# Two LSTMs in a decoder kernel: gates in two parts, cell and output gate transposed in place of h, inputs as three bf16 numbers, and a written-out order of half steps

## The chip, the cores and the metric

The kernel runs on one core of a Trainium2 chip. The metric is the device time of one execution in microseconds (us). The engines are named as in the profile: PE is TensorE, with its weight loads listed apart as PEld; DVE is VectorE, ACT is ScalarE, POOL is GpSimd, and SP issues most of the DMAs. A name such as L612 is a line of the kernel before.

## The reference, cut to what matters

The whole program is a decoder of four layers, each with self attention, cross attention and a feed-forward part, over x of 8 batches x 112 steps x 256. The change lies in the first sublayer. Its queries and keys come out of two LSTMs that read the same normalised x. Each has 256 units, so 1024 gate columns, and runs 112 steps one after the other:

```python
xW = jnp.einsum('bsd,gd->sbg', x, Wih) + b
def step(carry, xt):
    h, c = carry
    gates = xt + h @ Whh.T
    i, f, g, o = jnp.split(gates, 4, axis=-1)
    c = jax.nn.sigmoid(f) * c + jax.nn.sigmoid(i) * jnp.tanh(g)
    h = jax.nn.sigmoid(o) * jnp.tanh(c)
    return ((h, c), h)
...
hq = _lstm(hidden_states, Wih_q, Whh_q, b_q)
hk = _lstm(hidden_states, Wih_k, Whh_k, b_k)
```

Everything is float32. What follows (two small MLPs, attention, the other eleven sublayers) is untouched by the change.

## The kernel before, in words

`decoder` calls the twelve sublayers one after the other. `l0_attn` (L517) normalises x, transposes it (`ln_T_mm`), runs `lstm` (L559), then makes the values (L533, L534) and the attention. All instructions are issued through a tile framework that places the waits and, unless told otherwise, picks each engine's order by its own priorities.

In `lstm` a step's 8 batches x 1024 gate columns are laid out so that all 128 partitions work. `_gates` (L72) permutes the weights' columns at build time: column block j (0 to 3) of 256 columns holds 64 units of each gate, in the order i, f, o, g. A matmul with 32 stationary columns puts block j on partitions 32j to 32j + 31, so four matmuls fill a PSUM tile g of 128 x 256 (line L612, loops over the two halves c of h and the four blocks j). The 8 batches use 8 of the 32 partitions of each block.

The input part, xW, is made in blocks of 16 steps. `inputs(m, l, half)` (L580) multiplies 128 rows (8 batches x 16 steps) by 512 of the 1024 columns on PE and adds the bias on DVE into the SBUF tile `xw` (L585). `from_inputs(t, l)` (L587) brings the rows of step t into a fresh g: its stationary operand `pick[:, t % 16, :]` is a 0/1 matrix that selects 8 of the 128 rows (L590). PE does float32 matmuls as two instructions each, and here the moving operand is float32, 256 columns wide.

A time step of one LSTM (l = 0 is q, 1 is k) is then: 16 matmul instructions of h into g (L612); the inputs of the next step into the other g (L621, two PSUM buffers per LSTM); one sigmoid over 192 columns (L623) and one tanh over 64 (L624) on ACT; three DVE operations for the cell (L629 to L632); tanh of the cell on ACT (L634); h = o * tanh(c) on DVE (L636), with batches on partitions; DVE's transpose of 32 x 32 blocks, which gives hT with units on partitions (L638), the next step's stationary operand; and POOL's copy of its 8 batch columns to `hs` (L639), which keeps all steps. The two LSTMs are independent and alternate. The first 16 steps' inputs are made ahead of the loop; the other 24 blocks of 512 columns (`later`, L603) go one after every fourth step (L640).

Of the kernel before, what the change touches and what calls it, by code (L numbers as in the profile page):

```python
# [22 lines left out]
BF16 = mybir.dt.bfloat16  # L23
AF = mybir.ActivationFunctionType
ALU = mybir.AluOpType
AX = mybir.AxisListType
ET = mybir.EngineType
PSUM = bass.MemoryType.PSUM

P = 128  # L30
S, NB, D = 112, 8, 256
T = S * NB
# [39 lines left out]
def _gates(w):  # L72

    i, f, g, o = np.split(w, 4, axis=0)
    a = np.stack([i, f, o, g]).reshape(4, 2, 4, 32, *w.shape[1:])
    return np.moveaxis(a, 2, 0).reshape(1024, *w.shape[1:])


# [11 lines left out]
def _weights(inp):  # L90
    def g(layer):
        return lambda name: inp[f"{layer}_{name}"]

    a, xa, f = g("L0_attn"), g("L0_xattn"), g("L0_ffn")
    blobs = [
        [("l0a_ih_q", _fm(_gates(a("Wih_q")).T))],
        [("l0a_hh_q", _fm(_gates(a("Whh_q")).T))],
        [("l0a_ih_k", _fm(_gates(a("Wih_k")).T))],
        [("l0a_hh_k", _fm(_gates(a("Whh_k")).T))],
        [("l0a_b_q", _row(_gates(a("b_q")))), ("l0a_b_k", _row(_gates(a("b_k"))))],  # L100
# [228 lines left out]
class _Kernel:  # L329
# [229 lines left out]
    def lstm(self, hs, xs, ps0):  # L559

        nc, tc = self.nc, self.tc
        G = range(4)
        whh = [self.w("l0a_hh_q", 2), self.w("l0a_hh_k", 2)]
        wih = [self.w("l0a_ih_q", 2), self.w("l0a_ih_k", 2)]  # L570
        bias = [self.w("l0a_b_q"), self.w("l0a_b_k")]
        pick = self.c("pick").rearrange("p (r m) -> p r m", r=16)
        with tc.tile_pool(name="ps_lstm", bufs=2, space=PSUM) as ps, tc.tile_pool(
            name="lstm", bufs=2
        ) as work, tc.tile_pool(name="lstm_c", bufs=1) as cpool:

            xw = self.t(cpool, [P, 2, S // 16, 1024], "xw")
            cell = [self.t(cpool, [P, 64], f"cell{l}") for l in range(2)]

            def inputs(m, l, half):  # L580
                cols = slice(512 * half, 512 * half + 512)
                pm = self.t(ps0, [P, 512], "mm")
                steps = [xs[:, k, m, :, :].rearrange("p b r -> p (b r)") for k in range(2)]
                self.mm(pm, [(x, wih[l][:, k, cols]) for k, x in enumerate(steps)])
                nc.vector.tensor_tensor(xw[:, l, m, cols], pm, bias[l][:, cols], ALU.add)  # L585

            def from_inputs(t, l):  # L587
                g = self.t(ps, [P, 256], f"g{l}")
                for j in G:
                    nc.tensor.matmul(  # L590
                        g[32 * j : 32 * j + 32, :],
                        pick[:, t % 16, :],
                        xw[:, l, t // 16, 256 * j : 256 * j + 256],
                        start=True,
                        stop=t == 0,
                        skip_group_check=True,
                    )
                return g

            for l in range(2):  # L600
                for half in range(2):
                    inputs(0, l, half)
            later = [(m, l, half) for m in range(1, S // 16) for l in range(2) for half in range(2)]  # L603
            gs = [from_inputs(0, l) for l in range(2)]
            hT = [None, None]
            for t in range(S):
                for l in range(2):
                    g = gs[l]
                    if t > 0:
                        for c in range(2):  # L610
                            for j in G:
                                nc.tensor.matmul(  # L612
                                    g[32 * j : 32 * j + 32, :],
                                    hT[l][:, c, :],
                                    whh[l][:, c, 256 * j : 256 * j + 256],
                                    start=False,
                                    stop=c == 1,
                                    skip_group_check=True,
                                )
                    if t + 1 < S:  # L620
                        gs[l] = from_inputs(t + 1, l)  # L621
                    sg = self.t(work, [P, 256], f"sg{l}")
                    nc.scalar.activation(sg[:, :192], g[:, :192], AF.Sigmoid)  # L623
                    nc.scalar.activation(sg[:, 192:], g[:, 192:], AF.Tanh)  # L624
                    ig, fg, og, gg = (sg[:, 64 * i : 64 * i + 64] for i in range(4))
                    if t == 0:
                        nc.vector.tensor_tensor(cell[l], ig, gg, ALU.mult)
                    else:
                        nc.vector.tensor_tensor(cell[l], cell[l], fg, ALU.mult)  # L629
                        tmp = self.t(work, [P, 64], f"tmp{l}")  # L630
                        nc.vector.tensor_tensor(tmp, ig, gg, ALU.mult)
                        nc.vector.tensor_tensor(cell[l], cell[l], tmp, ALU.add)  # L632
                    th = self.t(work, [P, 64], f"th{l}")
                    nc.scalar.activation(th, cell[l], AF.Tanh)  # L634
                    h = self.t(work, [P, 64], f"h{l}")
                    nc.vector.tensor_tensor(h, og, th, ALU.mult)  # L636
                    hT[l] = self.t(work, [P, 2, 32], f"hT{l}")
                    nc.vector.transpose(hT[l].rearrange("p c b -> p (c b)"), h)  # L638
                    nc.gpsimd.tensor_copy(hs[:, t, l, :, :], hT[l][:, :, :NB])  # L639
                if t % 4 == 2 and later:  # L640
                    inputs(*later.pop(0))

    def l0_attend(self, hs, vv):
        nc, tc, w = self.nc, self.tc, self.w
# [1352 lines left out]
```

## Time and profile before

| | |
|---|---|
| median of 3 runs | 2508.41 us (2505.84 to 2514.92) |
| the profiled execution | 2510.18 us, span of its instructions 2508.4 us |
| mean granted TensorE clock | 0.933 |
| busy over the span: PE, PEld, DVE, ACT, POOL | 2223.4, 1343.6, 1460.0, 834.6, 212.9 us |
| first input product of the LSTMs ready (L585) | 25.8 us |
| first product from h (L612) to last copy to hs (L639) | 34.6 to 433.1 us |
| matmuls of h (L612) | 3552 instructions of 384 ns |
| matmuls of the inputs into g (L590) | 1792 of 379 ns |
| sigmoid (L623), tanh (L624), tanh of the cell (L634) | 224 each, 331, 218 and 258 ns |
| h (L636), its transpose (L638), POOL's copy (L639) | 224 each, 225, 245 and 217 ns |

The duration of a matmul in such a table runs from its start until its result is written; matmuls overlap, so busy time overstates what PE does. In the timeline each row gives start, length, engine, line, operation, the tile written and the tiles read, the shape, and in brackets how long the engine had idled and what released it. Rows that follow one another are merged (x16), with the time from the first start to the last end.

### The profile page before, as it was taken

Reading aid. Unit: us, or ns where it says so; the run is one execution under the profiler, and the core shown is the slowest. Engines: PE = TensorE matmul, PEld = TensorE weight load, DVE = VectorE, ACT = ScalarE, POOL = GpSimd, SP = SyncE. Lnnn points to the kernel's source line nnn. Section 1 sums busy time; section 2 is a strip of 40 time slices with the busy share of each in tenths; the row PEclk is TensorE's granted clock in tenths of the full one; section 3 lists DMA queues with packets and bytes.
Section 4 is the critical chain, followed back from the end, with each engine's and each line's share of the span. In section 5 each row is a group of like instructions: output and inputs, shape, how many; then the busy total and the mean of one; then the engine's idle time right before and its main releaser. Section 6 shows DMA issues by size and latency. Waiting matters only on the chain.

```text
span 2508.4 us, 43509 instructions
## 1 busy us (share of the span) xinstructions
PE 2223.4 (89%) x17192; PEld 1343.6 (54%) x17192; DVE 1460.0 (58%) x3879; ACT 834.6 (33%) x2276; POOL 212.9 (8%) x412
## 2 busy tenths in 40 slices
PE   6999999989989889999998887899999999799942
PEld 3444444657655656655666444456655556556622
DVE  4555656555544656763588664767660042656698
ACT  2333333111221246751012122367521111356621
POOL 0111111000001110000112231100000000100000
PEclk9999999786899999999999997999999999899966
DMA  4000001000010000001000001000111000000000
GB/s 182 2 2 2 2 19 63 1 17 1 17 51 1 14 18 2 18 18 42 34 1 34 18 18 59 34 2 1 52 51 50 35 17 1 1 1 2 2 0 15
DMA packets 10731, 56.42 MB, mean 22 GB/s; under 512 B 1833, under 2 KB 3625, under 8 KB 5536
## 3 DMA queue, kind: packets, MB, share of 16 engines
q1 hardware_dynamic: 8304, 45.03, 5.0%
q0 software_dynamic: 2080, 7.07, 0.8%
q8 instruction: 137, 2.24, 0.4%
q10 hardware_dynamic: 144, 1.54, 0.1%
q14 instruction: 66, 0.54, 0.1%
HBM read 52.69 MB, written 0.92 MB: 21 GB/s over the span
## 4 chain that ended last, share of the span: by engine, by line
PE 67%; DVE 21%; issue 5%; ACT 4%; DMA 1%; POOL 1%; DVEq 0%; ACTq 0%; POOLq 0%
PE mm L378 33%; PE gu L378 6%; PE g L612 6%; PE tr L1031 6%; PE sc L378 5%; PE av L378 3%; PE av L1047 2%; DVE xnm L1021 2%; DVE rot L1326 1%; ACT sg L623 1%; PE s L378 1%; ACT th L634 1%; DVE hT L638 1%; PE tr L477 1%; DVE h L636 1%
## 5 line engine op out<-in xcount | busy, mean ns | idle before, releaser
L612 PE MATMUL g<-w,hT 128*32 128x256 f32 x3552 | 237.4, 384 | 25.8 <-DVE hT L638 24.4
L1024 ACT ACTIVATE xe<-sc,xnm 112x375 f32<-112x375 f32 x384 | 215.6, 580 | 29.1 <-DVE xnm L1021 29.1
L1031 PEld LDWEIGHTS tr<-cst,xe 112*125 112x125 f32 x1152 | 157.2, 187 | 108.8 <-ACT xkT L982 30.0
L378 PE MATMUL mm<-xnT,w 128*128 128x448 f32 x432 | 191.3, 580 | 20.3 <-DVE qT L1329 4.5
L1031 PE MATMUL tr<-cst,xe 112*125 112x112 f32 x1152 | 197.8, 291 | 11.4 <-DVE xoT L1074 6.5
L1021 DVE TENSOR_REDUCE xnm<-sc 112x1 f32<-112x375 f32 x384 | 184.4, 541 | 29.2 <-PE sc L378 29.0
L378 PE MATMUL mm<-hT,w 128*128 128x448 f32 x512 | 193.0, 539 | 0.0
L612 PEld LDWEIGHTS g<-w,hT 128*32 128x32 f32 x3552 | 95.7, 109 | 167.5 <-DVE hT L638 124.6
L1039 DVE COPY xeT<-tr 125x336 f32<-125x336 f32 x192 | 97.4, 507 | 98.1 <-PE tr L1031 90.5
L378 PEld LDWEIGHTS mm<-hT,w 128*128 128x128 f32 x512 | 97.1, 190 | 94.4 <-issue 94.4
L378 PEld LDWEIGHTS mm<-xnT,w 128*128 128x128 f32 x432 | 80.5, 199 | 109.1 <-issue 55.8
L590 PE MATMUL g<-xw,cst 128*32 128x256 f32 x1792 | 138.7, 379 | 0.0
L378 PE MATMUL mm<-w,oT 128*112 128x256 f32 x416 | 119.8, 445 | 21.2 <-DVE oT L1506 13.7
L378 PE MATMUL mm<-w,hT 128*112 128x256 f32 x576 | 132.6, 389 | 0.0
L1037 ACT COPY xeT<-tr 125x336 f32<-125x336 f32 x192 | 85.3, 444 | 127.6 <-PE tr L1031 127.6
L378 PE MATMUL gu<-xnT,w 128*128 128x448 f32 x320 | 124.4, 544 | 1.7 <-DVE hT L1171 1.2
L378 PEld LDWEIGHTS mm<-w,hT 128*112 128x112 f32 x576 | 103.6, 182 | 27.6 <-issue 4.9
L378 PEld LDWEIGHTS mm<-w,oT 128*112 128x112 f32 x416 | 82.9, 208 | 52.4 <-DVE oT L1506 14.9
L623 ACT ACTIVATE sg<-g 128x192 f32<-128x192 f32 x224 | 74.2, 331 | 105.2 <-PE g L612 93.4
L634 ACT ACTIVATE th<-cell 128x64 f32<-128x64 f32 x224 | 57.7, 258 | 147.0 <-DVE cell L632 146.9
L455 DVE TENSOR_TENSOR x<-mm,x 112x256 f32<-112x256 f32 x64 | 27.1, 423 | 126.2 <-PE mm L378 126.2
L636 DVE TENSOR_TENSOR h<-sg,th 128x64 f32<-128x64 f32 x224 | 50.4, 225 | 84.9 <-ACT th L634 84.9
(375 smaller groups left out, 3744.5 us busy)
## 6 DMA issues: line engine op xcount, KB each, us to landing
w<-in_w SPq DMA_DIRECT2D x35, 1024.0 KB, 4.9
raw<-in_wq POOLq DMA_DIRECT2D x3, 1024.0 KB, 5.2
wi<-in_wint POOLq DMA_DIRECT2D x3, 768.0 KB, 5.9
w<-in_w SPq DMA_DIRECT2D x2, 896.0 KB, 16.6
w<-in_w SPq DMA_DIRECT2D x2, 768.0 KB, 4.1
ctxT<-in_ctxT ACTq DMA_DIRECT2D x1, 1500.0 KB, 7.8
cx<-in_ctx POOLq DMA_DIRECT2D x1, 1500.0 KB, 20.9
w<-in_w SPq DMA_DIRECT2D x2, 512.0 KB, 3.5
```

The source lines that it names most:

```text
L378: self.nc.tensor.matmul(out, lhsT, rhs, start=i == 0, stop=i == len(pairs) - 1)
L590: nc.tensor.matmul(g[32 * j : 32 * j + 32, :], pick[:, t % 16, :], xw[:, l, t // 16, 256 * j : 256 * j + 256], start=True, stop=t == 0, sk ...
L612: nc.tensor.matmul(g[32 * j : 32 * j + 32, :], hT[l][:, c, :], whh[l][:, c, 256 * j : 256 * j + 256], start=False, stop=c == 1, skip_group ...
L623: nc.scalar.activation(sg[:, :192], g[:, :192], AF.Sigmoid)
L634: nc.scalar.activation(th, cell[l], AF.Tanh)
L636: nc.vector.tensor_tensor(h, og, th, ALU.mult)
L1021: nc.vector.tensor_reduce(nm, sc, AX.X, ALU.max, negate=True)
L1024: nc.scalar.activation(e, sc, AF.Exp, bias=nm, accum_out=sums[b][:, at : at + 1])
L1031: nc.tensor.transpose(tp[:CH, i * S : (i + 1) * S], e[:, i * CH : (i + 1) * CH], self.ident[:S, :S])
L1037: nc.scalar.copy(eT, src)
L1039: nc.vector.tensor_copy(eT, src)
L1047: nc.tensor.matmul(avs[b][32 * j : 32 * j + 32, c * S : (c + 1) * S], values[b % 2][:CH, i, 4 * c + j, :], eTs[b, c, j][:, i, :], start=i ...
```

## The change

It does five things, all of them for the LSTMs.

1. The gates' order in a block becomes g, i, f, o, and each g splits into two PSUM tiles of 128 columns in banks of their own: part 0 with g and i, part 1 with f and o. The products of h run part by part, so that part 0 is finished first. ACT does four operations of 64 columns in place of one of 192 and one of 64. Each of the four tiles (two LSTMs, two parts) has one buffer.
2. h is no longer transposed. DVE transposes the cell and the output gate instead, tanh is taken of the transposed cell, and h is formed with units on partitions, on 2 x 8 columns. The stationary operand of h's products has 8 columns in place of 32.
3. The inputs xW are stored as a sum of three bf16 numbers, hi, mid and lo, which POOL splits off after DVE's bias add (two copies, two subtractions). `pick` is bf16, and `from_inputs` does three bf16 matmuls for each block and part in place of one float32 matmul for each block. `xw` is a ring of two tiles for each LSTM.
4. The later input products come in 96 pieces of 128 columns in place of 24 of 512: one in each half step of l = 0, and one more in l = 1 every eighth step, until they are done.
5. The order of PE, DVE and ACT is written out (`manual_schedule`): half step n is step n // 2 of LSTM n % 2, and `state`, the last part of a half step (tanh of the cell and h), is issued within the next half step, behind that one's first two activations and its tmp. POOL's order is left to the framework.

```diff
-    a = np.stack([i, f, o, g]).reshape(4, 2, 4, 32, *w.shape[1:])
+    a = np.stack([g, i, f, o]).reshape(4, 2, 4, 32, *w.shape[1:])
...
-        with tc.tile_pool(name="ps_lstm", bufs=2, space=PSUM) as ps, tc.tile_pool(
+        with tc.tile_pool(name="ps_lstm", bufs=1, space=PSUM) as ps, tc.tile_pool(
...
+            pick = self.t(cpool, [P, 16, 32], "pick", BF16)
+            nc.vector.tensor_copy(pick, self.c("pick").rearrange("p (r m) -> p r m", r=16))
...
-            def inputs(m, l, half):
-                cols = slice(512 * half, 512 * half + 512)
-                pm = self.t(ps0, [P, 512], "mm")
+            def inputs(m, l, cols):
+                pm = self.t(ps0, [P, 512], "mm")[:, : cols.stop - cols.start]
...
-                nc.vector.tensor_tensor(xw[:, l, m, cols], pm, bias[l][:, cols], ALU.add)
+                if (m, l) not in xws:
+                    xws[m, l] = self.t(work, [P, 3, 1024], f"xw{l}", BF16)
+                hi, mid, lo = (xws[m, l][:, i, cols] for i in range(3))
+                x = self.t(work, [P, 512], "x")[:, : cols.stop - cols.start]
+                nc.vector.tensor_tensor(x, pm, bias[l][:, cols], ALU.add)
+                nc.gpsimd.tensor_copy(hi, x)
+                nc.gpsimd.tensor_tensor(x, x, hi, ALU.subtract)
+                nc.gpsimd.tensor_copy(mid, x)
+                nc.gpsimd.tensor_tensor(lo, x, mid, ALU.subtract)
+
+            def product(g, lhsT, rhs, l, part, start, stop):
+                for j in G:
+                    at = 256 * j + 128 * part
+                    nc.tensor.matmul(
+                        g[32 * j : 32 * j + lhsT.shape[1], :], lhsT, rhs[:, at : at + 128],
+                        start=start, stop=stop, skip_group_check=True,
+                    )
 
             def from_inputs(t, l):
-                g = self.t(ps, [P, 256], f"g{l}")
...
+                gs = [self.t(ps, [P, 512], f"g{l}{part}")[:, :128] for part in range(2)]
+                for part, g in enumerate(gs):
+                    for i in range(3):
+                        xw = xws[t // 16, l][:, i, :]
+                        product(g, pick[:, t % 16, :], xw, l, part, i == 0, t == 0 and i == 2)
+                return gs
...
-            later = [(m, l, half) for m in range(1, S // 16) for l in range(2) for half in range(2)]
...
+            later = [
+                (m, l, slice(128 * q, 128 * q + 128))
+                for m in range(1, S // 16) for l in range(2) for q in range(8)
+            ]
+            hT, turned = [None, None], [None, None]
+
+            def state(t, l):
+
+                cT, oT = turned[l]
+                th = self.t(work, [P, 2, NB], f"th{l}")
+                nc.scalar.activation(th, cT[:, :, :NB], AF.Tanh)
+                hT[l] = self.t(work, [P, 2, NB], f"hT{l}")
+                nc.vector.tensor_tensor(hT[l], oT[:, :, :NB], th, ALU.mult)
+                nc.gpsimd.tensor_copy(hs[:, t, l, :, :], hT[l])
+
+            with tc.manual_schedule(engines={ET.PE, ET.DVE, ET.Activation}):
+
+                gs = [from_inputs(0, 0), None]
+                for n in range(2 * S):
+                    t, l = n // 2, n % 2
+                    for part, g in enumerate(gs[l]):
+                        for c in range(2):
+                            if t > 0:
+                                product(g, hT[l][:, c, :], whh[l][:, c, :], l, part, False, c == 1)
+                    ga, gb = gs[l]
+                    if n + 1 < 2 * S:
+                        gs[1 - l] = from_inputs((n + 1) // 2, 1 - l)
...
+                    nc.scalar.activation(flat[:, :64], ga[:, :64], AF.Tanh)
+                    nc.scalar.activation(flat[:, 64:128], ga[:, 64:], AF.Sigmoid)
+                    tmp = self.t(work, [P, 64], f"tmp{l}") if t > 0 else cell[l]
+                    nc.vector.tensor_tensor(tmp, ig, gg, ALU.mult)
+                    if n > 0:
+                        state((n - 1) // 2, 1 - l)
+                    nc.scalar.activation(flat[:, 128:192], gb[:, :64], AF.Sigmoid)
+                    nc.scalar.activation(flat[:, 192:], gb[:, 64:], AF.Sigmoid)
                     if t > 0:
                         nc.vector.tensor_tensor(cell[l], cell[l], fg, ALU.mult)
...
                         nc.vector.tensor_tensor(cell[l], cell[l], tmp, ALU.add)
...
-                    nc.vector.tensor_tensor(h, og, th, ALU.mult)
-                    hT[l] = self.t(work, [P, 2, 32], f"hT{l}")
-                    nc.vector.transpose(hT[l].rearrange("p c b -> p (c b)"), h)
-                    nc.gpsimd.tensor_copy(hs[:, t, l, :, :], hT[l][:, :, :NB])
-                if t % 4 == 2 and later:
-                    inputs(*later.pop(0))
+                    turned[l] = [self.t(work, [P, 2, 32], f"{i}T{l}") for i in "co"]
+                    nc.vector.transpose(turned[l][0].rearrange("p c b -> p (c b)"), cell[l])
+                    nc.vector.transpose(turned[l][1].rearrange("p c b -> p (c b)"), og)
+                    if later and t > 16 * later[0][0] - 18 and (l == 0 or t % 8 == 4):
+                        inputs(*later.pop(0))
+                state(S - 1, 1)
```

## The prediction

> **What bounds the kernel now.** I read the windows view first. The change touches one stage only, the two LSTMs, whose recurrence runs from 34.6 to 433.1 us; columns are length, then busy time (and count) of PE, PE's weight loads, DVE, ACT, POOL, then granted clock, DMA share, GB/s.
>
> ```profile
> 34.60:433.10 398.50, 372.69 (x5420) 171.26 (x5421) 239.69 (x1137) 154.85 (x666) 48.03 (x221) 1.00 0.04 12
> ```
>
> PE looks 94% busy, but a matmul's record holds its pipeline latency. So I went on to the timeline, which shows one whole time step (start, length, engine, line):
>
> ```profile
> 106.67 1.07 PE L612 MATMUL g<-w,hT 128*32 128x256 f32 x16 [0.26 <-DVE hT L638]
> 107.56 0.61 PE L590 MATMUL g<-xw,cst 128*32 128x256 f32 x8
> 107.87 0.33 ACT L623 ACTIVATE sg<-g 128x192 f32<-128x192 f32 x1 [0.40 <-PE g L612]
> 108.09 0.22 ACT L624 ACTIVATE sg<-g 128x64 f32<-128x64 f32 x1
> 108.23 0.23 DVE L629 TENSOR_TENSOR cell<-cell,sg 128x64 f32<-128x64 f32 x1
> 108.37 0.22 DVE L631 TENSOR_TENSOR tmp<-sg 128x64 f32<-128x64 f32 x1
> 108.63 0.22 DVE L632 TENSOR_TENSOR cell<-cell,tmp 128x64 f32<-128x64 f32 x1
> 108.94 0.26 ACT L634 ACTIVATE th<-cell 128x64 f32<-128x64 f32 x1 [0.63 <-DVE cell L632]
> 109.23 0.23 DVE L636 TENSOR_TENSOR h<-sg,th 128x64 f32<-128x64 f32 x1 [0.38 <-ACT th L634]
> 109.59 0.24 DVE L638 STREAM_TRANSPOSE hT<-h 128x64 f32<-128x64 f32 x1
> 109.89 1.07 PE L612 MATMUL g<-w,hT 128*32 128x256 f32 x16 [0.23 <-DVE hT L638]
> ```
>
> Each link starts as the one above ends: latency of one LSTM's chain sets the step, 109.89 - 106.67 = 3.22 us; the other LSTM runs in its gaps. So a half step (one LSTM, one step) costs 1.61 us. 111 x 3.22 = 357 us. The rest is the later input products (L584), 24 blocks of 512 columns:
>
> ```profile
> 112.27 0.61 PE L590 MATMUL g<-xw,cst 128*32 128x256 f32 x8
> 112.81 1.98 PE L378 MATMUL mm<-w,xs 128*128 128x512 f32 x4
> 114.73 0.42 PE L612 MATMUL g<-w,hT 128*32 128x256 f32 x4
> ```
>
> Matmuls from hT began at 109.89, 111.38 (gaps alternate 1.49 and 1.73), so the next was due at 113.11; it began at 114.73: 1.62 us, times 24 = 39 us. 357 + 39 = 396 against 398.5 measured.
>
> Last I looked for POOL beside DVE, since the change gives POOL work:
>
> ```profile
> 2151.98 1.13 POOL L1739 TENSOR_TENSOR eT<-eT,cst 112x448 f32<-112x448 f32 x1 [5.77 <-ACT eT L1737]
> 2152.36 1.23 DVE L1739 TENSOR_TENSOR eT<-eT,cst 112x448 f32<-112x448 f32 x1 [2.04 <-ACT eT L1737]
> ...
> L1739 DVE TENSOR_TENSOR eT<-eT,cst x8: 606/650/1225, 2146.4 to 2186.4; 112x448 f32<-112x448 f32 x8
> ```
>
> The same DVE instruction takes 0.61 us alone and 1.23 us when it meets POOL's: it ends 0.48 us, its streaming time, after POOL's ends at 2153.11.
>
> **What the Trainium skill says.** "GPSIMD Engine Reference", Specifications: POOL's SBUF interfaces are shared with DVE, and DVE instructions with two SBUF inputs contend. The lines above agree, with total exclusion. "TensorEngine Tiling (Array Packing)", Key Properties: changing the tiling mode drains TensorE. The trace agrees: 112.81 is 0.09 us after the 128x32 matmuls have streamed out, and the way back costs 0.09 again. "TensorE: Matmul & The Clock Gate", Part 1: a warm matmul of N columns takes N/2.4 ns + 2.5, and starts are never under 25 ns apart. The first agrees (bf16 128x128 of L1884 start every 56 ns), the second not: four column tiles start 7 ns apart here, in rounds of 216 ns for 256 fp32 columns (two passes each) and of 96 ns for the 112 columns of L1752. "ScalarE: Activation LUTs", What ACT_TABLE_LOAD costs: neighbouring ACTIVATEs overlap by 93 ns. The trace has L624 to L634, 32.95 to 33.05, so 64 columns issue every 0.105 us. Nor does tanh beside sigmoid reload a table within the loop.
>
> **Part by part.** *Half step without input piece.* From hT to ACT the old chain takes 107.87 - 106.67 = 1.20 us, four rounds of 0.216 in it. The first half of the gates needs four rounds of 0.109: 0.77. Tanh, then sigmoid, then tanh of the other LSTM's cell follow at 0.105 each, so the last starts at +0.21; it has 16 columns (0.217 us; 8 columns take 0.21 at L386), plus 0.03 to DVE as at L629: +0.46. The product h has 16 columns (0.17; small DVE rows of L389 to L392 take 0.16) plus 0.06 to PE as now: 0.23. Since PE's next half step waits for this h, and h waits behind this half step's first gates, the loop is 0.77 + 0.46 + 0.23 = 1.46 us, 0.15 less.
>
> Work beside it: tanh of the cell stood after three DVE links; now the forget gate (second half, +0.44), two cell operations (0.25, 0.26, 0.26) and the cell's transpose (0.33 with ACT's wait) make it ready at +1.54, and its turn in ACT's queue is at 1.46 + 0.21 = 1.67. It is hidden with 0.13 to spare (past that, each 0.1 us costs 128 x 0.1 = 13 us); the output gate's transpose lies in the same cover. The transpose of h leaves the chain. PE: eight rounds of 0.109 and 0.024 start, six bf16 rounds of 0.056 (was 0.432): 1.23 of 1.46, hidden. The gates' PSUM tiles are single now: the inputs of half step n + 1 overwrite the gates of n - 1, whose last sigmoid ends 0.77 + 0.44 + 0.105 + 0.22 = 1.53 us after their products began, 0.07 into half step n, and the inputs are due 0.9 into it: no wait. No DMA is added or moved, and POOL's copy to hs stays.
>
> *Half step with piece.* 96 pieces of 128 columns take the place of 24 of 512. PE: 1.23 + drain 0.09 + weight load 0.107 + four fp32 matmuls of 0.109 + drain 0.09 = 1.96 us; the next half step's products are queued behind this, so PE is the bound there, +0.35 on 1.61. DVE's add of the piece stands ahead of the next tmp in DVE's queue but is done 0.6 us before that is due: nothing.
>
> Sum: 128 x -0.15 = -19; 96 x 0.35 = +34; the old blocks -39. Loop **-24.5 us**.
>
> *Start.* POOL splits the first four 512-column pieces, each two copies (0.62 as L1062's 512 columns) and two subtractions (0.26 + 512 x 1.95 ns from 761 at 256 and 1136 at 448 columns, so 1.26): 3.76 us, four in a row from 26.5, done at 41.5. The second LSTM's inputs wait for that, and with the half-step order the first h too: first product from h near 42.9 instead of 34.9. **+8 us**; nothing hides it, it can't be below zero, and at half POOL's price it is +1.
>
> *POOL in the loop.* A 128-column piece costs it two copies of 0.29 and two subtractions of 0.51, 1.6 us in a step of 3.4: throughput is no issue. But tmp, h and both cell operations have two SBUF inputs and wait while a subtraction holds the port. No row shows 64-column operations against a 128-column subtraction. Zero is one end: a gain is excluded, and L631 runs unharmed beside L639's 16-column copy. The other is all four POOL operations blocking to their end (the one-column L1915 met a copy and took 0.34 instead of 0.15). Walking the queues through a period with these durations: windows of 0.3 us per subtraction cost the loop 4 us in all, 0.4 us 12, all four operations 34. Most hits fall in the piece's half step, where DVE has 0.5 us to spare. I take **+7**, toward the short windows, since some of POOL's 0.26 us is fixed and holds no port.
>
> Sum: -24.5 + 8 + 7 = -9.5. The profiled execution took 2510.2 us (span 2508.4), 1.8 above the median 2508.4; against its own time 2500.7, as a median **2499 us**. What is late next: PE in piece half steps, h's wait in the others.
>
> **Rivals.** *POOL costs nothing* (chance 0.33): for L631 beside L639, 16 columns though; -16.5, 2492; with the drains hidden also, 96 x 0.18 less, 2475. *POOL paces the loop* (0.16), slower: all its four operations hold the port, tmp or h waits each piece. The gain left to lose is 24.5 - 8 = 16.5, so it decides from 16.5 / 96 = 0.17 us a piece; at 34 us (0.35 a piece) 2508.4 + 17.5 = 2526. For it: L1739, L1915; against: L392 runs its 0.16 us beside L909. *bf16 rounds cost as much as fp32's* (0.06): 32-column weight loads or the instruction stream (112 PE instructions a half step, 48 now) hold them at 0.109. PE then needs 1.55 and 2.28: 128 x 0.09 + 96 x 0.32 = +42, 2541. Against: L1752. *The order doesn't shorten the chain* (0.05): another wait keeps 1.61; +19, 2518.
>
> **How the numbers follow.** Forecast 0.40 (POOL's cost between 3 and 16: 2495 to 2508). A measurement here can tell about 0.5%, 12.5 us, from no change. Faster: the first rival and a quarter of the forecast, 0.43. Slower: most of the second, the third, half of the fourth, 0.20. Range 2478, part of the drains hidden, to 2530, past the second rival; left out are the cheap end and the bf16 rival.
>
> **What would show it.** Starts of the h products 1.46 us apart without, 1.96 with a piece; those after a piece longer by POOL's hold; TENSOR_TENSOR over 0.3 us in the loop wherever POOL subtracts; bf16 rounds of 0.056; first product from h near 43 us; the loop's end near 424. A plain half step above 1.55, or pieces above 2.2, make the forecast wrong.

## The result and the profile after

The changed kernel takes 2513.71 us (median of 20 runs, 2511.26 to 2520.40) beside 2507.88 us for the kernel before (20 runs, 2505.84 to 2514.92): a ratio of 1.0023, with a 95% interval of 1.0016 to 1.0030. It is slower by 0.23%, less than the 0.5% taken above as no change, and 14.7 us above the forecast of 2499. Its profiled execution took 2513.32 us, 3.1 above that of before, where the sum of the forecast said 9.5 below. L numbers are now lines of the changed kernel.

The windows view over the LSTMs of the changed kernel, from the first product of h to the last copy into `hs` (columns as before: length, then busy time and count of PE, PE's weight loads, DVE, ACT, POOL, then clock, DMA share, GB/s):

```profile
43.40:435.40 392.00, 367.93 (x12805) 322.39 (x12798) 274.19 (x1431) 159.36 (x1111) 183.08 (x608) 1.00 0.05 14
```

The loop begins 8.8 us later (43.4 against 34.6; forecast +8) and is 392.0 us long in place of 398.7 (34.6 to 433.3, where the last copy ends): -6.7, where -24.5 + 7 = -17.5 had been forecast. PE's count is the other thing to see: 12805 matmuls and as many weight loads, against 5420.

The timeline of one plain half step of the changed kernel, the link that the forecast had to get right:

```profile
407.28 1.07 PE L602 MATMUL g<-w,hT 128*8 128x128 f32 x32
...
408.03 0.22 ACT L648 ACTIVATE sg<-g 128x64 f32<-128x64 f32 x1 [0.81 <-PE g L602]
...
408.15 0.22 ACT L649 ACTIVATE sg<-g 128x64 f32<-128x64 f32 x1
408.16 0.52 PE L602 MATMUL g<-xw,pick 128*32 128x128 bf16 x24
408.26 0.22 ACT L628 ACTIVATE th<-cT 128x16 f32<-128x16 f32 x1
408.40 0.22 DVE L651 TENSOR_TENSOR tmp<-sg 128x64 f32<-128x64 f32 x1 [0.38 <-ACT sg L649]
...
408.58 0.18 DVE L630 TENSOR_TENSOR hT<-oT,th 128x16 f32<-128x16 f32 x1
...
408.81 0.41 PE L602 MATMUL g<-w,hT 128*8 128x128 f32 x8
```

Read it as the old step was read. First tanh 0.75 us after PE's start (forecast 0.77), tanh of the cell 0.23 later (0.21), h 0.32 after that begins (0.25: 0.217 + 0.03), PE 0.23 later (0.23). 408.81 - 407.28 = 1.53, not 1.46. The bf16 matmuls are as forecast: from one round of four to the next 0.056 us in the trace.

For all half steps I took the starts of the first tanh (L648, 224 of them) and their differences, the first three left out. 94 with an input piece behind the products: 1.958 us on average (forecast 1.96). 126 plain ones: 1.601 on average, median 1.572; among the 44 that follow neither a piece nor its neighbour the median is 1.529. So plain half steps are late in three ways. The 1.53 is the first. The second, and third, are in these lines. The timeline of the changed kernel while POOL splits a piece:

```profile
105.03 0.47 POOL L595 TENSOR_TENSOR x<-x,xw 128x128 f32<-128x128 f32 x1
105.13 0.44 DVE L657 TENSOR_TENSOR cell<-cell,sg 128x64 f32<-128x64 f32 x1
...
105.56 0.29 POOL L596 CAST xw<-x 128x128 bf16<-128x128 f32 x1
105.61 0.32 DVE L658 TENSOR_TENSOR cell<-cell,tmp 128x64 f32<-128x64 f32 x1
```

DVE's cell operation takes 0.44 us in place of 0.22 while POOL subtracts, and the next one 0.32 beside POOL's cast: the cost that the forecast took at 7 us. And the timeline of the changed kernel after the last piece (372.2 us):

```profile
382.24 0.40 PE L602 MATMUL g<-w,hT 128*8 128x128 f32 x8
...
382.98 0.12 PEld L602 LDWEIGHTS g<-w,hT 128*8 128x8 f32 x8 [0.63 <-issue]
382.98 0.41 PE L602 MATMUL g<-w,hT 128*8 128x128 f32 x8 [0.34 <-issue]
```

PE stands still for 0.63 us in the middle of the 32 weight loads of one half step. "issue" means that nothing in the profile held it: no engine, no buffer. There are 13 such stalls, all after 376 us and most of them 3.5 to 4.0 us apart. After 376 us the trace has one packet of queue q8, the instructions' own, of 16 KB, every 3.3 to 4.0 us, and each of the 13 stalls ends 1.2 to 1.5 us after such a packet has ended. A half step has 112 PE instructions now and 48 before, so 256 of them go by in 3.5 us. Before the experiments this was a suspicion, no more.

### The profile page after: what moved, and what is told of

The parts are those of the page before. It is cut to its first block, busy times and chain, and to the rows that moved or that the text cites. A ratio compares the mean times of both kernels' runs of the same rounds, so it can differ in the third digit from the quotient of the medians.

```text
span 2511.2 us, 59212 instructions
## 1 busy us (share of the span) xinstructions
PE 2218.5 (88%) x24616; PEld 1497.9 (60%) x24616; DVE 1495.8 (60%) x4176; ACT 839.2 (33%) x2725; POOL 360.9 (14%) x812
## 4 chain that ended last, share of the span: by engine, by line
PE 66%; DVE 21%; issue 5%; ACT 4%; POOL 3%; DMA 1%; ACTq 0%; DVEq 0%; POOLq 0%
PE mm L378 32%; PE g L602 6%; PE gu L378 6%; PE tr L1054 6%; PE sc L378 5%; PE av L378 3%; PE av L1070 2%; DVE xnm L1044 1%; DVE rot L1349 1%; DVE hT L630 1%; PE s L378 1%; POOL x L595 1%; ACT sg L648 1%; PE tr L477 1%; PE tr L378 1%
## 5 line engine op out<-in xcount | busy, mean ns | idle before, releaser
L602 PE MATMUL g<-w,hT 128*8 128x128 f32 x7104 | 237.5, 274 | 22.3 <-DVE hT L630 15.0
L602 PEld LDWEIGHTS g<-w,hT 128*8 128x8 f32 x7104 | 171.9, 90 | 56.3 <-DVE hT L630 41.2
L648 ACT ACTIVATE sg<-g 128x64 f32<-128x64 f32 x224 | 50.0, 223 | 246.6 <-PE g L602 246.6
L602 PE MATMUL g<-xw,pick 128*32 128x128 bf16 x5376 | 120.2, 220 | 9.6 <-POOL xw L596 4.2
L651 DVE TENSOR_TENSOR tmp<-sg 128x64 f32<-128x64 f32 x222 | 58.0, 261 | 99.8 <-ACT sg L649 99.4
L602 PEld LDWEIGHTS <-pick 128*32 128x32 bf16 x5376 | 102.2, 98 | 12.9 <-issue 12.8
```

Of the source, the lines that this page charges most:

```text
L602: nc.tensor.matmul(g[32 * j : 32 * j + lhsT.shape[1], :], lhsT, rhs[:, at : at + 128], start=start, stop=stop, skip_group_check=True,)
L648: nc.scalar.activation(flat[:, :64], ga[:, :64], AF.Tanh)
```

## The experiments

Each ratio is to the kernel before, from runs on the same chip, with its 95% interval. "Against the changed kernel" means the difference of the two ratios times 2508 us; the changed kernel's is 1.0023. By the intervals such a difference is uncertain by 2 to 5 us. The table has the half steps of all runs, by the starts of the first tanh as above; a stall is a step of over 0.13 us from the start of one weight load to the next within a run of them, put down to "issue", from 48.5 us to the end of the loop.

| kernel | PE instructions, plain half step | plain: median / mean us | with piece: mean us | stalls |
|---|---|---|---|---|
| changed | 112 | 1.572 / 1.601 | 1.958 | 13 |
| e1 h ahead of tmp | 112 | 1.555 / 1.593 | 1.958 | 17 |
| e2 fp32 inputs | 96 | 1.512 / 1.537 | 2.060 | 2 |
| e3 casts only | 112 | 1.534 / 1.580 | 1.958 | 15 |
| e4 no pieces | 112 | 1.529 / 1.595 | none | 59 |
| e5 tanh of the cell second | 112 | 1.441 / 1.546 | 1.986 | 32 |
| e6 = e4, fourth round | 128 | 1.805 / 1.845 | none | 109 |
| e7 gates in one bank | 88 | 1.991 / 1.994 | 1.980 | 0 |
| e8 = e2 + e5 | 96 | 1.395 / 1.445 | 2.060 | 8 |
| e9 = e4, two rounds | 96 | 1.528 / 1.533 | none | 0 |
| e10 = e8, blocks of 512 | 96 | 1.396 / 1.437 | 3.364 (block) | 16 |
| e11 changed, blocks of 512 | 112 | 1.529 / 1.690 | 3.252 (block) | 13 |
| e12 h turned | 112 | 1.954 / 1.958 | 1.974 | 1 |

My first theory was that h comes late because tmp stands ahead of it on DVE, and that the stalls are PE's instruction stream; the rivals were POOL, and a wait for the tanh of the cell.

**e1: h issued ahead of tmp.**

```diff
+                    if n > 0:
+                        state((n - 1) // 2, 1 - l)
                     tmp = ...
                     nc.vector.tensor_tensor(tmp, ig, gg, ALU.mult)
-                    if n > 0:
-                        state((n - 1) // 2, 1 - l)
```

> The product h of the other LSTM is issued on DVE ahead of tmp, not behind it. Theory (the chain: a plain half step is 1.53 us and not 1.46 because h starts 0.16 to 0.18 us behind tmp, 0.54 us after the gates' first tanh where 0.46 was forecast): plain half steps fall to about 1.46 us wherever no stall is in them, 128 x 0.07 = 9 us at most, so -5 to -9 us against the changed kernel, near 2506. Rival (PE's instruction stream paces the plain half steps: 112 PE instructions each, about 256 per 3.5 us): those after the last piece, 379 us on, stay at 1.53 on average or get longer stalls in exchange, and the gain is under 4 us. Second rival (h was not late on DVE but waits for tanh of the cell): no change.

Measured: 2515.57 us, 1.0023 (1.0013 to 1.0034), no difference from the changed kernel. From the start of the tanh of the cell to the start of h it is still 0.306 us (median; 0.325 in the changed kernel). So tmp costs 0.02 us and my theory of the missing 0.07 fell; the second rival, that h waits for the tanh, was right. But the tanh is not the slow part: it takes 0.217 us, as forecast. The time is lost behind it. In the medians, h starts 0.088 us after the tanh's end here and 0.108 in the changed kernel, and it was 0.032 before the change. Source views show what stands in this gap (count, then ns min/median/max, first and last start; DVEq is DVE's sequencer, and EVENT_SEMAPHORE an instruction that only waits). Before the change, h has none of these, and the transpose behind it has them:

```profile
L636 DVE TENSOR_TENSOR h<-sg,th x224: 202/225/227, 33.3 to 432.5; 128x64 f32<-128x64 f32 x112
...
L638 DVEq EVENT_SEMAPHORE  x220: 21/50/50, 40.9 to 432.7; - x110
```

In the changed kernel they stand ahead of h:

```profile
L630 DVEq EVENT_SEMAPHORE  x268: 21/98/242, 42.9 to 434.7; - x134
```

The reason is in the program. The first operation to write a buffer of `hT` must wait until PE and POOL have read what was in it. That was the transpose, and it is h now. By the semaphores in the trace, h waited for ACT alone before and waits for PE, POOL, ACT and DVE's own transposes now. Where a DVE operation itself holds the wait for ACT, it starts 0.024 us after ACT's semaphore (tmp in the changed kernel, 210 times); where a wait instruction ahead of it holds it, 0.079 us (h in e1).

**e2: fp32 inputs.** The three bf16 numbers and the split are undone, `pick` is fp32 again; halves, order and pieces stay.

```diff
-                nc.gpsimd.tensor_copy(hi, x)
...
-                nc.gpsimd.tensor_tensor(lo, x, mid, ALU.subtract)
+                nc.vector.tensor_tensor(xws[m, l][:, cols], pm, bias[l][:, cols], ALU.add)
...
-                    for i in range(3):
-                        xw = xws[t // 16, l][:, i, :]
-                        product(g, pick[:, t % 16, :], xw, l, part, i == 0, t == 0 and i == 2)
+                    product(g, pick[:, t % 16, :], xws[t // 16, l], l, part, True, t == 0)
```

> The inputs are one fp32 number again (no split on POOL, one fp32 product per block in place of three bf16 ones); order and halves of the gates stay. Theory (POOL's port costs about 6 us, the start 8.5, the instruction stream 3 to 4): the first product from h comes near 35 us (was 43.4), DVE operations over 0.3 us in the loop vanish, PE has 96 instructions a half step and not 112, so the stalls shrink; a piece half step is longer by two fp32 rounds in place of six bf16 ones, 0.10 us x 95 = +10. Sum -8.5 - 6 - 3 + 10 = -7 us, near 2506. Rival (the three bf16 numbers pay for themselves): piece half steps go to 2.2 us and plain ones to 1.6 as PE becomes their bound, and the time rises by 5 us or more.

Measured: 2507.36 us, 0.9996 (0.9988 to 1.0005), so 7 us below the changed kernel, as summed. No DVE operation of the loop is over 0.3 us long; the first product of h comes at 34.0; pieces cost 0.10 more; two stalls are left. The mean of the plain half steps after a piece is 1.522, against 1.607: over 76 of them 6.5 us, most of it POOL's, since the changed kernel has no stall before its last piece.

**e3: casts in place of subtractions.** POOL writes `hi`, `mid` and `lo` as three casts of x; both subtractions are left out.

```diff
-                nc.gpsimd.tensor_tensor(x, x, hi, ALU.subtract)
                 nc.gpsimd.tensor_copy(mid, x)
-                nc.gpsimd.tensor_tensor(lo, x, mid, ALU.subtract)
+                nc.gpsimd.tensor_copy(lo, x)
```

> POOL makes three casts per piece and no subtraction (the middle and low numbers are then copies of the high one: the subtractions are left out). Theory (the two subtractions hold the port that DVE's two-input operations need; the casts don't): the long DVE operations in the loop vanish, -5 to -6 us there, and the start is shorter by about eight subtractions of 1.16 us less what other work hides, 5 to 9 us: -11 to -15 in all. Rival (POOL's casts hold it too): DVE operations over 0.3 us stay beside the casts, and the loop gains under 2 us.

Measured: 2506.68 us, 0.9988 (0.9981 to 0.9994), 9 us below the changed kernel; the sum of 11 to 15 was too high. In the profile the loop begins 8.0 us earlier, as summed, and is 3.4 us shorter, not 5 to 6. In the groups by line and shape, up to the last piece, the cell's two operations average 217 and 225 ns here, 237 and 252 ns in the changed kernel; tmp averages 252 ns here, 268 there, and 225 in e2. So without the subtractions the cell's operations run free. This doesn't clear the casts: a cell operation starts beside one only 15 times in this loop, and tmp, which meets them, is held up. The plain half steps after a piece average 1.562 us, about halfway from the changed kernel's 1.607 to e2's 1.522; e11 shows the casts at work. The stalls after the last piece stay (15), which the subtractions therefore don't cause.

**e4: no pieces.** All later pieces are left out.

```diff
-                for m in range(1, S // 16) for l in range(2) for q in range(8)
+                for m in range(1, 1) for l in range(2) for q in range(8)
...
-                        xw = xws[t // 16, l][:, i, :]
+                        xw = xws[0, l][:, i, :]
```

> All later input pieces are left out; every time step reads the inputs of the first 16. What is left is 224 plain half steps with the full chain. Theory (chain 1.53, the instruction stream nearly as slow): the loop from the first product of h to the last copy takes 224 x 1.53 = 343 us plus stalls of some 0.13 us a half step on average, 343 to 372 us against 392. Rival A (chain alone, no stalls from the stream except at the end): 343 us and no half step over 1.58. Rival B (the stream is the bound, and pieces only gave it time to catch up): half steps of 1.6 us or more on average, 360 us or more, with PE standing still inside a run of weight loads every 256 instructions.

Measured: 2476.67 us, 0.9879 (0.9862 to 0.9897). With no pieces and no POOL split in the loop, the median is 1.529, the chain, and the mean 1.595: 59 stalls, spread over the whole loop, most of them 3.4 to 4.0 us apart. Rival A, the chain alone, is out; the mean is close to rival B's 1.6. On average 256 instructions take 1.595 x 256/112 = 3.65 us.

**e6 and e9: more and fewer PE instructions.** e6 adds to e4 a fourth round of bf16 products, of a zero row; e9 leaves the round of the low numbers out.

```diff
-                    for i in range(3):
-                        xw = xws[0, l][:, i, :]
-                        product(g, pick[:, t % 16, :], xw, l, part, i == 0, t == 0 and i == 2)
+                    for i in range(4):
+                        xw = xws[0, l][:, i % 3, :]
+                        row = zeros if i == 3 else pick[:, t % 16, :]
+                        product(g, row, xw, l, part, i == 0, t == 0 and i == 3)
```

> The kernel without pieces with a fourth round of bf16 products per half, of a zero row: 16 more PE instructions a half step, 128 in place of 112, and 0.11 us more of PE work, which is 1.34 of 1.53 then. (It leaves out the same as the kernel without pieces.) Theory (the stream paces: 256 instructions in 3.65 us): a half step goes from 1.595 on average to 1.78 to 1.83, 224 x 0.21 = +40 to +50 us, 2516 to 2526. Rival (the stalls come from something else, the chain paces): 0 to +5 us, 2477 to 2482.

> The kernel without pieces with two rounds of bf16 products a half in place of three: 96 PE instructions a half step, where 112 gave 1.595 us on average and 128 gave 1.845. (It leaves out the same as the kernel without pieces, and the low numbers of the inputs.) Theory (a half step takes the longer of its chain, 1.53, and its share of the instruction stream, 256 in 3.67 us): 96 x 3.67/256 = 1.38, below the chain, so 1.53 on average with almost no stalls: 224 x 0.065 = -14 us, near 2463. Rival (time goes with the number of instructions all the way down): 1.38 to 1.45, 2428 to 2444. Rival (stalls have another cause): 1.595, no change.

Measured: e6 2533.67 us, 1.0089 (1.0072 to 1.0106); e9 2461.27 us, 0.9809 (0.9789 to 0.9829). With 96, 112 and 128 instructions a half step takes 1.533, 1.595 and 1.845 us on average. The step from 112 to 128 is 0.25 us where the products' own work is 0.11; that from 96 to 112 is 0.06. Below 112 the chain sets the time, above it the stream: 1.845 x 2 = 3.69 us for 256 instructions in e6. The timeline of e6 shows it, PE alone:

```profile
302.76 0.33 PEld L604 LDWEIGHTS g<-w,hT 128*8 128x8 f32 x15 [0.20 <-DVE hT L633]
302.76 0.62 PE L604 MATMUL g<-w,hT 128*8 128x128 f32 x14
304.00 0.70 PE L604 MATMUL g<-w,hT 128*8 128x128 f32 x17 [0.62 <-issue]
304.00 0.41 PEld L604 LDWEIGHTS g<-w,hT 128*8 128x8 f32 x16 [0.91 <-issue]
```

At 128 instructions a half step, two half steps are 256, and the stop falls in the middle of the 32 weight loads of every second half step: here, and at 299.98 and 307.74 in the same trace. This settles that the number of PE instructions is what the stalls hang on. What in the fetching takes 3.7 us for 16 KB, of which a packet's own transfer is 0.9 to 1.4, no run here shows.

**e5: tanh of the cell second on ACT.** It goes ahead of the input gate's sigmoid, and h ahead of tmp.

```diff
                     nc.scalar.activation(flat[:, :64], ga[:, :64], AF.Tanh)
+                    if n > 0:
+                        state((n - 1) // 2, 1 - l)
                     nc.scalar.activation(flat[:, 64:128], ga[:, 64:], AF.Sigmoid)
...
-                    if n > 0:
-                        state((n - 1) // 2, 1 - l)
```

> On ACT the tanh of the other LSTM's cell comes second, after this half step's first tanh and ahead of its sigmoid, and h comes ahead of tmp on DVE. Theory (two limits close together: the chain of h at 1.53 us, and PE's instruction stream, 256 instructions in some 3.65 us as in the kernel without pieces): the chain falls by one ACT issue, 0.11, to 1.42, but a piece and a plain half step together are 232 instructions in 3.5 us already, so stalls inside runs of weight loads appear all through the loop and take most of it: -3 to -8 us against the changed kernel, 2506 to 2511. Rival A (only the chain bounds plain half steps): -0.11 x 128 = -14 us, 2500. Rival B (tanh of the cell isn't ready that early and holds ACT's queue): slower than the changed kernel by up to 10 us.

Measured: 2505.55 us, 0.9978 (0.9969 to 0.9987), 11 us below the changed kernel by the ratios; of the two profiled executions the loop differs by 3.6 us. By the ratios that is between the theory's range and rival A, by the profiles inside the theory's range. The median falls to 1.441, and stalls appear between pieces too: 32, from 203 us on. The chain got shorter, and the stream took a good part of that back.

**e8: fp32 inputs and tanh of the cell second**, the two edits above together.

> fp32 inputs (no split, no bf16) together with the tanh of the cell second on ACT and h first on DVE. With 96 PE instructions a half step the stream isn't near its limit (one stall in the fp32 kernel's loop). Theory: plain half steps fall from 1.51 to about 1.42 us, those with a piece stay at 2.07: -0.09 x 128 = -11 us against the fp32 kernel, 2496, 12 us faster than the kernel before. Rival A (the chain of the cell, ready at best 1.5 us after the first tanh, takes the place of h's): plain half steps 1.47 to 1.51, -5 us at most, 2502 or more. Rival B (ACT's order costs what it gives): no change, 2507.

Measured: 2495.90 us, 0.9933 (0.9918 to 0.9948), 16 us below e2 by the ratios; by the profiles the loop is 11.6 shorter, the expected 11. The timeline of e8 shows the same links with one ACT operation less in them:

```profile
402.12 1.06 PE L595 MATMUL g<-w,hT 128*8 128x128 f32 x32
...
402.87 0.22 ACT L639 ACTIVATE sg<-g 128x64 f32<-128x64 f32 x1 [0.68 <-PE g L595]
...
402.99 0.21 ACT L619 ACTIVATE th<-cT 128x16 f32<-128x16 f32 x1
...
403.29 0.18 DVE L621 TENSOR_TENSOR hT<-oT,th 128x16 f32<-128x16 f32 x1 [0.28 <-ACT th L619]
...
403.52 0.73 PE L595 MATMUL g<-w,hT 128*8 128x128 f32 x20
```

0.75 + 0.12 + 0.30 + 0.23 = 1.40 us. With DVE idle for 0.28 us ahead of h, h still starts 0.09 us after the tanh's end: the wait instructions ahead of it are the same as in e1.

**e10: e8 with the later inputs in 24 blocks of 512 columns**, one in every fourth step.

```diff
-                (m, l, slice(128 * q, 128 * q + 128))
-                for m in range(1, S // 16) for l in range(2) for q in range(8)
+                (m, l, slice(512 * q, 512 * q + 512))
+                for m in range(1, S // 16) for l in range(2) for q in range(2)
...
-                    if later and t > 16 * later[0][0] - 18 and (l == 0 or t % 8 == 4):
+                    if later and t > 16 * later[0][0] - 18 and l == 0 and t % 4 == 1:
```

> fp32 inputs, tanh of the cell second, and the later inputs in the 24 blocks of 512 columns of before in place of 96 pieces. Theory (a piece of 128 costs PE two drains, a weight load and four matmuls, 0.73 us, of which a plain half step hides only what PE has free, 0.07 at a chain of 1.40; a block of 512 pays drains and load once): PE needs 1.33 + 0.29 + 4 x 0.436 = 3.36 us there, against four half steps with a piece at 2.06; 24 x (4 x 2.06 - 3.36 - 3 x 1.40) = -16 us against the same kernel with pieces, near 2480. Rival (DVE's add of 512 columns, 0.7 us, now stands ahead of tmp or h): +0.3 to +0.5 us a block, 10 us of it lost, 2490. Rival (longer plain stretches run into the instruction stream: 96 instructions in 1.38 at best): plain half steps of 1.45 on average, +5 us, 2485.

Measured: 2483.22 us, 0.9894 (0.9873 to 0.9914): 1.06% faster than the kernel before, the fastest of those that leave nothing out. A half step with a block takes 3.364 us, as worked out (3.36); DVE's long add isn't felt. The stream is, as the second rival said: the mean of the plain half steps is 0.041 us above their median, 8 us over the loop, and 3.0 of it is one stall beside a transfer of weights.

**e11: the changed kernel with these blocks**, the split on POOL kept.

> The changed kernel with the later inputs in 24 blocks of 512 columns again in place of 96 pieces of 128; the split on POOL stays. Theory of the forecast (PE's bound): 1.23 + 0.29 + 4 x 0.436 = 3.26 us in a half step with a block, 1.73 over a plain one, 24 x 1.73 = 41.5, and the pieces cost 96 x 0.43 = 41: no change from that. What else changes: three plain half steps in four run without a piece's pause for the instruction stream, so they go to 1.60 on average, 96 x 0.06 = +5, and POOL's subtractions of 1.16 us meet DVE's operations after each block, 24 x 0.5 = +12 in place of +6. Sum +5 to +12 us, 2519 to 2526. Rival (neither the stream nor POOL is felt): within 3 us of the changed kernel.

Measured: 2540.26 us, 1.0122 (1.0102 to 1.0143), 25 us above the changed kernel and not 5 to 12. PE's part is right (3.252 us a block, 3.26 expected), and the stream is hardly felt between blocks: there are 13 stalls, 10 of them after 409 us. POOL is what I had too small. The timeline of e11 after a block:

```profile
202.02 0.61 POOL L596 CAST xw<-x 128x512 bf16<-128x512 f32 x1
202.05 0.66 DVE L657 TENSOR_TENSOR cell<-cell,sg 128x64 f32<-128x64 f32 x1
...
202.71 1.16 POOL L597 TENSOR_TENSOR xw<-x,xw 128x512 bf16<-128x512 f32 x1
202.75 1.21 DVE L658 TENSOR_TENSOR cell<-cell,tmp 128x64 f32<-128x64 f32 x1
202.93 0.22 ACT L648 ACTIVATE sg<-g 128x64 f32<-128x64 f32 x1 [0.87 <-PE g L602]
...
204.27 0.21 ACT L628 ACTIVATE th<-cT 128x16 f32<-128x16 f32 x1 [0.99 <-DVE cT L660]
```

A cast of 512 columns holds a cell operation of 0.22 us for 0.66, and the subtraction behind it holds the next for 1.21; each is over 0.08 to 0.09 us after POOL's operation ends. ACT stands idle for 0.99 us until the cell is ready for its tanh, and this half step takes 2.62 us. The Trainium skill, "GPSIMD Engine Reference", Specifications, says that POOL shares its SBUF interfaces with DVE, and that DVE operations with two SBUF inputs contend; the lines agree, to the whole length of the cast and of the subtraction. Pieces of 128 keep each such hold under 0.5 us, where the loop has slack for most of it.

**e7: both halves of the gates in one bank**, with each bf16 round 256 columns wide, meant as a test of the stream with 88 instructions.

```diff
-                gs = [self.t(ps, [P, 512], f"g{l}{part}")[:, :128] for part in range(2)]
+                g = self.t(ps, [P, 512], f"g{l}")[:, :256]
...
+                return g[:, :128], g[:, 128:]
```

> Both halves of the gates in one bank, so that each round of the inputs' bf16 product is 256 columns in place of two of 128: 88 PE instructions a half step in place of 112, PE's time about the same. Theory: stalls inside runs of weight loads after the last piece vanish (13 in the changed kernel), plain half steps there go to 1.53; piece half steps stay at 1.96, since PE's time sets them: -3 to -5 us, 2509 to 2511. Rival A (the stalls are not from the number of instructions): no change. Rival B (reading the first half holds up PE's writes of the second in the same bank): half steps of 1.7 us or more, +20 us.

Measured: 2561.88 us, 1.0191 (1.0174 to 1.0207). There are no stalls, but at these half steps there would be none anyway, so on the stream it says nothing. Its timeline shows why it is slow:

```profile
303.04 1.06 PE L602 MATMUL g<-w,hT 128*8 128x128 f32 x32
...
304.22 0.22 ACT L651 ACTIVATE sg<-g 128x64 f32<-128x64 f32 x1 [1.29 <-PE g L602]
```

The first tanh starts 1.18 us after PE, in place of 0.75. In the trace the matmuls raise ACT's semaphore once there, after the last of 32, and after the 16th in the changed kernel: with both halves in one tile and bank the program itself waits for both. It isn't rival B's mechanism, but its time. The run shows what finishing the first half early is worth: 0.43 us a half step.

**e12: h turned, as before the change.** Tanh and h are on 64 columns, then comes the transpose; the cell and the output gate aren't turned.

```diff
-                hT[l] = self.t(work, [P, 2, NB], f"hT{l}")
-                nc.vector.tensor_tensor(hT[l], oT[:, :, :NB], th, ALU.mult)
+                h = self.t(work, [P, 64], f"h{l}")
+                nc.vector.tensor_tensor(h, oT, th, ALU.mult)
+                full = self.t(work, [P, 2, 32], f"hT{l}")
+                nc.vector.transpose(full.rearrange("p c b -> p (c b)"), h)
+                hT[l] = full[:, :, :NB]
```

> h is turned again, as before the change, and not the cell and the output gate; all else stays (tanh and h on 64 columns, then a transpose ahead of the products). Theory (chain of one ordered half step: first tanh 0.75, tanh of the cell +0.23, h +0.31, transpose +0.36, products +0.30): 1.95 us where no piece is, and 2.0 with one, so +0.42 x 128 = +54 us, near 2566. Rival (the order leaves the transpose room beside other work): under +25 us.

Measured: 2561.89 us, 1.0210 (1.0190 to 1.0230), 47 us above the changed kernel, with plain half steps of 1.958 (forecast 1.95). Taking the transpose out of the chain works as forecast. h waits for ACT alone again, and the wait instructions are back at the transpose:

```profile
L632 DVEq EVENT_SEMAPHORE  x187: 21/21/50, 53.2 to 481.1; - x187
```

From the tanh's start to h's it is 0.29 us here, with 64 columns, and 0.325 in the changed kernel, with 16. These are two different sums: 0.258 for the tanh and 0.034 behind it here, 0.217 and 0.108 there. Fewer columns do shorten the tanh; the waits take more than that back.

## Why the prediction was wrong

It said 9.5 us faster for the profiled execution, and that is 3.1 slower: a miss of 12.6 (14.7 by the medians). By its own steps:

- **Plain half step 1.46: wrong, the largest term.** The step that failed is "it has 16 columns (0.217 us; 8 columns take 0.21 at L386), plus 0.03 to DVE as at L629: +0.46". The 0.217 is as measured; the 0.03 is 0.108. It was taken from a DVE operation that waits for ACT alone. But the sum took the transpose out of the chain whole, and the waits that stood ahead of it passed to h (e1). They were in the chain before, too: in the timeline of before, h ends at 109.46 and its transpose starts at 109.59, 0.13 us later, where one cell operation follows another by 0.03. Of the 0.108, tmp ahead of h is 0.02 (e1). The other links of the sum were right to 0.02. 126 x (1.53 - 1.46) = **+8.8 us**.
- **Instruction stream: left out, +3.2 us.** The third rival named it, but only as a way to slow the bf16 rounds, and as L1752 spoke against slow rounds it got a chance of 0.06. The rounds are at 0.056; the limit is on the number of instructions over several us, and a half step of 1.53 with 112 of them is already at it (e4, e6, e9). In the changed kernel the pieces hide it, since each takes 0.4 us and few instructions; after the last piece it shows. Of the 3.2 us, 1.7 are one long stall of 1.9 us at 377 us, while a transfer of weights (2 x 1024 KB) has the DMA engines; the instruction packets there are 6.8 us apart, and 3.8 before that. The DMA view of the changed kernel from 374 to 380 us (packets, MB, share of 16 engines):

```profile
q1 hardware_dynamic: 270, 1.96, 77.9%
q8 instruction: 1, 0.02, 1.0%
```

- **POOL +7: right in size, in part by luck.** The plain half steps behind a piece are 5.8 us over 1.53 in all. But the 7 leaned on short windows, with part of a subtraction holding nothing. In the traces a DVE operation that POOL holds is held until just past the end of POOL's, and casts hold as well (e11). For windows of 0.4 us the forecast's own walk gave 12 us, for all four operations 34; the loop's slack hid more than it assumed. e11 shows that the bound of 34 was no fancy: with operations of 512 columns 25 us are lost.
- **Half step with piece 1.96: right** (1.958), by PE's own work, as the sum had it. e11 and e10 repeat the sum for blocks, 3.252 and 3.364 us.
- **Old blocks -39, pieces +34:** at a plain half step of 1.53 a piece costs 0.43 and all 96 cost 41, so the pieces gained nothing over the blocks on PE. This is in the first item's difference, since it was counted by the half step.
- **Start +8: right**, +8.8 from the window view's 34.6 (the sum set out from 34.9). e2 gives it back: the first product of h at 34.0.
- **After the loop +1.1, not foreseen.** The values' products (L534) that follow had begun 1.9 us ahead of the loop's end before the change and begin 0.8 us ahead of it now, by the starts of their bias adds.

The sum: 8.8 + 3.2 - 1.2 (POOL 5.8, not 7) - 0.2 (pieces) + 0.9 (start) + 1.1 = 12.6. The mechanism that was forecast was right; of the 17.5 us that it was to gain in the loop, one link's 0.07 us, 126 times, took half, and a limit that wasn't priced another fifth. It had also said that a plain half step above 1.55 would make it wrong: the mean is 1.60.

Not settled: what the loop gains if only h's extra waits go (no run took them away with all else kept; their cost is read from the traces of e1 and e12), and how much of the 1.595 in e4 is single stalls and how much a steady limit, as 1.529 is so near it.

## What to carry to other kernels

Price a link of a dependency chain together with its waits: an operation that becomes the first to write a tile takes over the waits for those who read it. Where an edit cuts work into smaller instructions, multiply the engine's instructions per period too: a chain of 1.53 us with 112 PE instructions was at the limit here, and the same order with 96, one ACT operation less in the chain and blocks of 512 columns (e10) was 1.1% faster than the kernel before. An edit that hides its work on POOL has to be looked at for what DVE does at that moment.

## What the hardware showed that I had not expected

- In e6, with 128 PE instructions a half step, 256 of them took 3.45 to 4.02 us from stall to stall, 3.70 on average. Stalls away from a transfer of weights last from under 0.1 to 1.2 us (e4, e5, e6), and the profile puts them down to "issue".
- A DVE operation starts 0.024 us after ACT's semaphore when it holds the wait itself (tmp in the changed kernel), and 0.079 after it when a wait instruction ahead of it does (h in e1).
- POOL's casts from fp32 to bf16 can hold up a DVE operation with two SBUF inputs as its subtractions do: in e11 a cell operation took 0.66 us in place of 0.22 beside a cast of 0.61, and 1.21 beside a subtraction of 1.16. It goes the other way too: in the changed kernel a cell operation that starts 0.025 us after the second cast (L596) takes its usual 0.21 us, 77 times, and that cast takes 0.386 us in place of 0.289.
- While a transfer of 2 MB of weights ran, the next instruction packet came 6.8 us after the last, and PE stopped for 1.9 us. In e1, e2, e3, e5, e8 and e10 this transfer ran at other times, from 343 us in e10 to 372 in e1, and each time a stop of 1.0 to 3.0 us lies in it or ends within 0.2 us of its end, with packets 5.7 to 8.8 us apart there. In e7, e11 and e12 the packets were 5.0 to 7.7 us apart and PE did not stop. So where the stop occurs it moves with the transfer; that the transfer causes it is only argued, as no run kept this loop and left the transfer out of it.
